# A two-layer graph kernel: adjacency and code transposes moved from TensorE to DMA, and idle ticks behind the last gather

## The chip, the core and the metric

The kernel runs on one core of a Trainium2 chip. The metric is device time in microseconds (us), the median of several executions. One execution was also profiled; lines in the fences marked `profile` come from it. The engines are TensorE (PE; its weight loads are PEld), VectorE (DVE), ScalarE (ACT), GpSimd (POOL) and SyncE (SP), which here only issues DMAs.

## What is computed

There are 16 samples of 1024 nodes with 128 features, and a symmetric 0/1 adjacency matrix for each sample. Layer 0 is masked attention, layer 1 a three-stage GraphSAGE on a thinned ("dilated") adjacency:

```python
h = relu(layernorm(x))
q, k, v = (relu(h @ W.T + b) for W, b in ...)
logits = (q @ k.T) * adj - NEG * (1 - adj)
x = x + relu((softmax(logits) @ v) @ Wo.T + bo)

h = relu(layernorm(x))
adj_d = dilate(adj, nodemask)      # row by row: rows with over 10 neighbours lose most of them
for k in (1, 2, 3):                # deg: row sums of adj_d
    h = bn(relu(l2norm((adj_d @ h / deg) @ Wr[k] + h @ Wx[k] + b[k]))); hs.append(h)
x = x + concat(hs) @ Wl + bl
```

`dilate` is sequential: a row's removals also zero the columns. The kernel doesn't run it row by row. It bounds which nodes can keep neighbours, gathers the few rows of those nodes, and solves for them. At the end it tests its own assumptions (a 0/1 matrix, symmetric, a full diagonal, few enough such nodes); if one fails, a general program computes everything. The inputs here take the fast way.

## The kernel before

**Stages.** `fast` first runs attention, one *step* for each sample (16 steps, about 21 to 777 us), then finishes the last values (to about 788 us), then layer 1's first stage (to about 930 us) and its second and third. The dilation is woven into attention.

**Order of work.** The order on each engine is written by hand, in *ticks*. A step has 48 ticks (`TICKS`). `step(i)` issues one scores matmul pair every third tick (`scores`, L697: a 128×512 f32 block of logits) and in between quarters of the values matmuls of the half sample before (`values`, L713). `pace()` counts the ticks; at each it first runs what `clock.later` put off, then advances the generators in `agenda`, each with its list of ticks from `plan`. So the lists `AT_...` (L736 to L748) say when each piece of other work is emitted. Engines run what they are given in this order, and wait on semaphores for data and for free buffers; nothing is timed at run time. The SP queue too is in order.

**Loads.** `Dilation.load(b)` (L158 to L178) loads one 128×1024 f32 block row of the adjacency into `st` by SP's queue (L166, three buffers, `ST`), and ScalarE turns it into 0/1 bf16 in `ab` with row sums (L167), then counts the zeros in a second pass (L177; VectorE, L174, for the first two samples). A sample's eight block rows are loaded one step ahead, a piece every third tick (`AT_LOAD`: the block rows at ticks 1, 7, 13, 19, 25, 31, 37, 43). A load waits only for the pass that frees its `st` buffer.

**The mirror test.** `mirrors(b)` tests that `ab` is symmetric. For block row k, `mirror` (L180) transposes the blocks (j, k), j ≤ k, on TensorE into a PSUM bank (L186, 1 to 8 blocks of 128×128 bf16), and one tick later VectorE compares the bank with block row k, blocks 0 to k (L192); `odd` receives the count of differences. Ticks: `AT_MIRRORS`, one list for even and one for odd steps; the first entry is `count_loops`.

**The gather.** For every sample, `gather` (L284 to L328) has 13 pieces: four of one-hot comparisons (L291), a small matmul for row numbers (L296), the indirect DMA of 128 adjacency rows by POOL (L301), a suffix sum by VectorE (L305, `left`), the codes (L308, fp16 128×1024), eight TensorE transposes of the codes into PSUM (L312), two ScalarE evictions into `turned` (L316), a matmul of `turned` with the one-hot matrix (L320, `pq`), and three small operations on `pq`. Ticks: `AT_GATHER`, planned in odd steps for two samples. The first of the pair transposes at tick 11 of the following even step (59 − 48), the second at tick 41 of it (89 − 48).

**Beside these**, in each step: `project` of the next sample (transposes L598, Q, K and V by L676 with evictions L677 or L599 by ScalarE from a single `pm` bank), `bound` (L221), `store` of x2 rows by POOL's indirect DMAs (L540), and from step 5 on `solve`. The x tile of sample i + 2 is loaded at the head of a step (L651) into one of five buffers, and waits for an earlier sample's stored rows.

**The end.** Two pieces of the last gather, that of sample 15, run within the ticks after attention; its other pieces and the last `solve` run as `last_of_dilation` (L899) beside layer 1's first stage: `beside1` (L1054) advances it evenly over `TICKS1` = 120 ticks, 8 for each sample. `PIECES1` (L1051) is the number of pieces to spread. In that stage SP loads the x2 tiles (L840).

Of the kernel before, what the change touches and what calls it, by code (L numbers as in the profile page):

```python
# [8 lines left out]
BF = mybir.dt.bfloat16  # L9
H16 = mybir.dt.float16  # L10
I32 = mybir.dt.int32
AF = mybir.ActivationFunctionType
# [26 lines left out]
GROUP = 4  # L39
AB = 2  # L40
ST = 3
ONE_K = 2.0 ** 40
ZERO_K = 2.0 ** 126
ROUND = 2.0 ** 23
# [36 lines left out]
class Dilation:  # L81
# [7 lines left out]
    def __init__(self, tc, adj, accT, ones, jp, identf, pool, psum, rows, rows_psum, clock):  # L89

        self.nc, self.adj = tc.nc, adj
        nc = self.nc
        self.accT, self.ones = accT, ones
        self.pick = {}
        self.pool, self.psum, self.rows, self.rows_psum, self.put_off = pool, psum, rows, rows_psum, clock.later
        own = self.pool

        def const(name, shape, dtype=F32):
            return own.tile(shape, dtype, name=name, bufs=1)

        self.identf = identf
        self.identb, self.identh = (const(f"d_id{i}", [P, P], t) for i, t in enumerate((BF, H16)))
        for t in (self.identb, self.identh):
            nc.vector.tensor_scalar(t, jp, 0.0, None, op0=OP.is_equal)
        self.up = const("d_up", [P, P], BF)
        nc.vector.tensor_scalar(self.up, jp, 0.0, None, op0=OP.is_gt)
        self.after = const("d_after", [P, P], BF)
        nc.vector.tensor_scalar(self.after, jp, 0.0, None, op0=OP.is_lt)
        nc.vector.scalar_tensor_tensor(self.after, self.identb, BIG, self.after, op0=OP.mult, op1=OP.add)
        self.onesb = const("d_ones", [P, P], BF)  # L110
        nc.vector.memset(self.onesb, 1.0)
        self.onesf = const("d_onesf", [P, P])
        nc.vector.memset(self.onesf, 1.0)
        self.half = const("d_half", [P, 1], BF)
        nc.vector.memset(self.half, 0.5)
        self.one_k = const("d_one_k", [P, 1])
        nc.vector.memset(self.one_k, -ONE_K)
        ii = const("d_ii", [P, S], I32)
        nc.gpsimd.iota(ii, pattern=[[1, S]], base=1, channel_multiplier=0)
        self.iota = const("d_iota", [P, S], H16)  # L120
        nc.vector.tensor_copy(self.iota, ii)
        mi = const("d_mi", [P, NB], I32)
        nc.gpsimd.iota(mi, pattern=[[P, NB]], base=0, channel_multiplier=1)
        self.node = const("d_node", [P, NB])
        nc.vector.tensor_copy(self.node, mi)
        self.node32 = mi
        self.node16 = const("d_node16", [P, NB], H16)
        nc.vector.tensor_copy(self.node16, mi)
        self.first = [const(f"d_first{i}", [P, NB, 2], BF) for i in range(2)]
        self.away = [const(f"d_away{i}", [P, 2, NB, 3], BF) for i in range(2)]  # L130
        self.limits = [const(f"d_limits{i}", [P, NB, 2]) for i in range(2)]
        self.neghalf = const("d_neghalf", [P, 1], BF)
        nc.vector.memset(self.neghalf, -0.5)
        for t in self.away + self.first:
            nc.vector.memset(t, 1.0)

        self.deg = const("d_deg", [P, B, NB])
        self.zeros = const("d_zeros", [P, B, NB])
        self.odd = const("d_odd", [P, B, NB])
        self.loops = const("d_loops", [P, B])  # L140
        self.sizes = const("d_sizes", [P, B, 2])
        self.used = const("d_used", [P, B])
        self.code = const("d_code", [P, B, S], H16)
        self.own = const("d_own", [P, B, P], BF)
        self.dcode = const("d_dcode", [P, B])
        self.moved = const("d_moved", [P, B])
        self.kept_deg = const("d_kdeg", [P, B])
        self.slot = const("slot", [P, B, NB], I32)
        self.A = {}
        self.tail = False  # L150

    def bank(self, shape, dtype, own=False):
# [5 lines left out]
    def load(self, b):  # L158
# [5 lines left out]
        for k in range(NB):  # L164
# [12 lines left out]
                nc.scalar.activation(junk, st, AF.Exp, scale=-ZERO_K, accum_out=zeros)  # L177
            yield  # L178

    def mirror(self, b, k):  # L180

        nc = self.nc
        ab, diag = self.A[b]
        pt = self.bank([P, NB, P], BF)
        for j in range(k + 1):
            nc.tensor.transpose(pt[:, j, :], ab[:, j, k * P:(k + 1) * P], self.identb)  # L186
        n = (k + 1) * P // 2

        def compare():

            junk = self.rows.tile([P, NB, P], BF, name="junkv", bufs=1)
            nc.vector.scalar_tensor_tensor(junk.rearrange("p a b -> p (a b)")[:, :n],  # L192
                                           pt.rearrange("p a b -> p (a b)").bitcast(I32)[:, :n], 1.0,
                                           ab[:, k, :].bitcast(I32)[:, :n], op0=OP.mult, op1=OP.not_equal,
                                           accum_out=self.odd[:, b, k:k + 1])

        self.put_off(1, compare)

    def prepare(self, b):

# [83 lines left out]
    def gather(self, b):  # L284


        nc = self.nc
        used = self.used[:, b:b + 1]
        onehot = self.pool.tile([P, NB, S], H16, name="onehot", bufs=1)
        for k in range(NB):  # L290
            nc.vector.tensor_scalar(onehot[:, k, :], self.iota, self.pick[b - b % 2][:, b % 2, k:k + 1], None, op0=OP.is_equal)  # L291
            if k % 2:
                yield
        pi = self.bank([P, 1], F32)
        for k in range(NB):
            nc.tensor.matmul(pi, onehot[:, k, :P], self.node16[:, k:k + 1], start=(k == 0), stop=(k == NB - 1))  # L296
        yield
        row = self.pool.tile([P, 1], I32, name="row")
        nc.vector.tensor_scalar(row, pi, float(b * N), None, op0=OP.add)
        rows = self.pool.tile([P, N], F32, name="rows", bufs=1)  # L300
        nc.gpsimd.indirect_dma_start(out=rows, out_offset=None, in_=self.adj.rearrange("b n m -> (b n) m"),  # L301
                                     in_offset=bass.IndirectOffsetOnAxis(ap=row[:, 0:1], axis=0))
        yield
        left = self.pool.tile([P, N], H16, name="left", bufs=1)
        nc.vector.tensor_tensor_scan(left[:, ::-1], rows[:, ::-1], rows[:, ::-1], 0.0, op0=OP.add, op1=OP.bypass)  # L305
        yield
        codes = self.pool.tile([P, N], H16, name="codes", bufs=1)
        nc.vector.scalar_tensor_tensor(codes, rows, 1023.0, left, op0=OP.mult, op1=OP.add)  # L308
        yield
        pt = self.bank([P, NB, P], H16)  # L310
        for k in range(NB):
            nc.tensor.transpose(pt[:, k, :], codes[:, k * P:(k + 1) * P], self.identh)  # L312
        yield
        turned = self.pool.tile([P, NB, P], H16, name="turned", bufs=1)
        for h in range(2):
            nc.scalar.activation(turned[:, 4 * h:4 * h + 4, :], pt[:, 4 * h:4 * h + 4, :], AF.Copy)  # L316
            yield
        pq = self.bank([P, S], F32)
        for k in range(NB):
            nc.tensor.matmul(pq, turned[:, k, :], onehot[:, k, :], start=(k == 0), stop=(k == NB - 1))  # L320
        yield
        dg = self.pool.tile([P, P], BF, name="dg")
        nc.vector.scalar_tensor_tensor(dg, pq[:, :P], used, self.identf, op0=OP.mult, op1=OP.mult,
                                       accum_out=self.dcode[:, b:b + 1])
        nc.vector.tensor_scalar(self.own[:, b, :], dg, 512.0, None, op0=OP.is_gt)
        nc.vector.scalar_tensor_tensor(self.code[:, b, :P], pq[:, :P], used, self.up, op0=OP.mult, op1=OP.mult)
        nc.scalar.activation(self.code[:, b, P:], pq[:, P:], AF.Copy, scale=used)
        yield  # L328
# [184 lines left out]
def fast(ctx: ExitStack, tc: tile.TileContext, a, out, vp):  # L513
# [127 lines left out]
    with ExitStack() as s1:  # L641
# [110 lines left out]
        def plan(gen, start, ticks):  # L752
            agenda.append((gen, [start + t for t in ticks]))

        def solve_pieces(b0, b1):
            return 9 * ITER + 3 + 13 * (b1 - b0)

        def plan_step(i):
# [6 lines left out]
            else:  # L765
                late = lambda ticks: ticks
            plan(dil.bound(i), start, late(AT_BOUND[odd]))
            plan(dil.mirrors(i), start, late(AT_MIRRORS[odd]))
            if i + 1 < B:
                plan(project(i + 1), start, late(AT_PROJECT[odd]))  # L770
                plan(load_adj(i + 1), start, late(AT_LOAD))
# [120 lines left out]
                    H[b] = enter(b)  # L892
                _advance(H[b][1])
        clock.flush()
        assert all(gen is gathering[B - 1] for gen, ticks in agenda if ticks)
        dil.tail = True
    load_x2(2)

    def last_of_dilation():  # L899

        yield from gathering[B - 1]
        yield from dil.solve(LAST, B)

    def last_stores():
# [139 lines left out]
    with tc.tile_pool(name="ps1", bufs=2, space=PSUM, reuse_waits="tile") as ps:  # L1044
# [3 lines left out]
        checks = dil.verdict(a["nodemask"], vp, recips)  # L1048
        _advance(checks)

        tick, TICKS1, PIECES1 = 0, 8 * (B - 1), 13 + solve_pieces(LAST, B)  # L1051
        entering = iter(())

        def beside1():  # L1054
# [776 lines left out]
```

## Time and profile before

| | us |
|---|---|
| median of 3 runs | 1245.71 |
| lowest and highest | 1243.62 and 1247.72 |
| the profiled execution | 1249.27 |
| its span, first to last instruction | 1247.5 |
| TensorE busy in the span | 1101.4 (88%) |
| VectorE, ScalarE, POOL busy | 881.2, 727.6, 576.8 |
| transposes of adjacency blocks (L186), 576 of them | each 0.22 from start to end |
| transposes of codes (L312), 128 of them | each 0.22 to 0.31 |

How to read it: a line of the profile names engine, source line, operation, the tile written `<-` the tiles read, shapes and a count. In a timeline the first two numbers are start and duration, and `[x <-E]` says that the engine had been idle for x us until E. Consecutive matmuls overlap, so the spacing of their starts, not their durations, tells what they cost. Busy time is an average over stages with different limits; what a change in one stage is worth is read from that stage.

### The profile page before, as it was taken

The numbers are of one execution on the slowest core, as the hardware profiler recorded it, in microseconds if no ns is written. First come the engines' busy times: TensorE is split into PE (matmuls) and PEld (weight loads), VectorE is DVE, ScalarE is ACT, GpSimd is POOL, SyncE is SP. The second block draws the span as 40 slices with busy tenths as digits, with TensorE's granted clock in tenths as the row PEclk, the third lists the DMA queues.
The fourth block names the chain that finished last, engine by engine and source line by source line (L and its number), as shares of the span: only waits on it lengthen the run. The fifth ranks groups of instructions, "written<-read, shape, count | busy, mean of one in ns | idle before, by whom it ended". The sixth has DMA issues, their size and how long they took to land. (4 is left out here: it accounts for less than half of the span.)

```text
span 1247.5 us, 22348 instructions
## 1 busy us (share of the span) xinstructions
PE 1101.4 (88%) x7775; PEld 824.0 (66%) x7775; DVE 881.2 (71%) x2630; ACT 727.6 (58%) x1570; POOL 576.8 (46%) x1082
## 2 busy tenths in 40 slices
PE   4899899899899899899899798498769969999895
PEld 2567677566576676676566566477647858888673
DVE  5767568588788578678778778489866875666542
ACT  5578678677677777677677642266534542333221
POOL 0330752662652752752743605778300004777686
PEclk9899999999999999999999999699879989999797
DMA  6544334334334244244234301414000013778554
GB/s 201 154 132 136 97 128 151 124 116 131 111 114 150 86 140 149 86 137 151 85 122 135 112 25 55 120 47 111 1 1 1 1 35 99 232 218 239 164 180 124
DMA packets 118147, 143.45 MB, mean 115 GB/s; under 512 B 9212, under 2 KB 94088, under 8 KB 118024
## 3 DMA queue, kind: packets, MB, share of 16 engines
q1 hardware_dynamic: 106120, 110.78, 29.7%
q0 software_dynamic: 11904, 31.15, 7.7%
q8 instruction: 63, 1.03, 0.3%
q14 instruction: 60, 0.49, 0.1%
HBM read 113.39 MB, written 28.51 MB: 114 GB/s over the span
## 5 line engine op out<-in xcount | busy, mean ns | idle before, releaser
L713 PEld LDWEIGHTS po<-vw,e 128*128 128x128 f32 x2048 | 273.2, 194 | 65.8 <-issue 65.3
L713 PE MATMUL po<-vw,e 128*128 128x129 f32 x2048 | 307.0, 284 | 0.0
L697 PE MATMUL ps<-qT,kT 128*128 128x512 f32 x512 | 271.8, 614 | 0.8 <-ACT e L699 0.8
L700 DVE TENSOR_TENSOR e<-e,ab 128x512 f32<-128x512 f32 x256 | 177.3, 694 | 112.5 <-ACT e L699 110.8
L699 ACT ACTIVATE e<-ps 128x512 f32<-128x512 f32 x256 | 153.1, 598 | 106.0 <-PE ps L697 83.3
L540 POOL DMA_INDIRECT x_d<-xt,slot x128 | 144.2, 1127 | 38.8 <-issue 35.1
L167 ACT ACTIVATE ab<-st,d_one_k 128x1024 bf16<-128x1024 f32 x128 | 146.9, 1148 | 0.3 <-DMA st<-in_adj_dram 0.3
L576 POOL TENSOR_SCALAR ln_t<-ln_st 128x8 f32<-128x8 f32 x31 | 8.1, 260 | 289.7 <-DVE ln_st L569 231.8
L177 ACT ACTIVATE junk<-st 128x1024 bf16<-128x1024 f32 x112 | 118.3, 1056 | 0.0
L540 POOL DMA_INDIRECT y_d<-y,nodes x88 | 86.4, 982 | 29.0 <-issue 28.5
L722 ACT ACTIVATE o<-po,recips 128x128 f32<-128x128 f32 x128 | 46.8, 368 | 74.7 <-DVE recips L720 74.6
L697 PEld LDWEIGHTS ps<-qT,kT 128*128 128x128 f32 x512 | 78.6, 193 | 7.6 <-issue 3.1
L954 ACT ACTIVATE sq<-po 128x512 f32<-128x512 f32 x80 | 47.7, 596 | 57.5 <-PE po L945 51.9
L1000 ACT ACTIVATE r<-pt 128x512 f32<-128x512 f32 x74 | 44.4, 601 | 58.3 <-PE pt L988 58.3
L588 POOL TENSOR_SCALAR hn<-xt,ln 128x128 f32<-128x128 f32 x120 | 76.4, 649 | 1.6
L957 DVE TENSOR_REDUCE nrm<-sq 128x4 f32<-128x512 f32 x80 | 54.1, 676 | 31.4 <-ACT sq L954 27.8
L944 PE MATMUL po<-ws,r 128*128 128x128 f32 x512 | 75.4, 292 | 0.0
L305 DVE TENSOR_TENSOR_SCAN left<-rows 128x1024 f16<-128x1024 f32 x16 | 38.1, 2384 | 51.4 <-DMA rows<-in_adj_dram,row 51.4
L944 PEld LDWEIGHTS po<-ws,r 128*128 128x128 f32 x512 | 64.8, 198 | 12.8 <-issue 11.2
L1130 POOL COPY mark<-y 128x1 f32<-128x1 f32 x30 | 5.8, 193 | 145.8 <-DVE y L1005 143.0
L997 DVE BATCH_NORM_STATS2 stats<-r 128x6 f32<-128x512 f32 x74 | 50.9, 688 | 29.6 <-ACT r L1000 29.2
L588 POOL TENSOR_SCALAR hn<-xt 128x128 f32<-128x128 f32 x112 | 56.3, 514 | 27.0 <-PE pt L598 26.2
(300 smaller groups left out, 2435.2 us busy)
## 6 DMA issues: line engine op xcount, KB each, us to landing
st<-in_adj_dram SPq DMA_DIRECT2D x128, 512.0 KB
r<-y_d SPq DMA_DIRECT2D x22, 512.0 KB
xt<-x_d SPq DMA_DIRECT2D x16, 524.0 KB
xt<-in_x_dram SPq DMA_DIRECT2D x16, 512.0 KB
x<-x_d SPq DMA_DIRECT2D x16, 512.0 KB
out_dram<-r SPq DMA_DIRECT2D x11, 512.0 KB
x_d<-xt,slot POOLq DMA_INDIRECT x128
y_d<-y,nodes POOLq DMA_INDIRECT x88
```

Of the source, the lines that this page charges most:

```text
L167: nc.scalar.activation(ab[:, k, :], st, AF.Exp, bias=self.one_k, scale=ONE_K, accum_out=self.deg[:, b, k:k + 1])
L177: nc.scalar.activation(junk, st, AF.Exp, scale=-ZERO_K, accum_out=zeros)
L540: d = nc.gpsimd.indirect_dma_start(out=dst, out_offset=bass.IndirectOffsetOnAxis(ap=slots, axis=0), in_=src, in_offset=None)
L588: engine.tensor_scalar(hn[:, k, :], xt[:, k, :D], minus[:, k // 2, k % 2, None], rstd[:, k // 2, k % 2, None], op0=OP.add, op1=OP.mult)
L697: nc.tensor.matmul(p, K[b][:, k * P:(k + 1) * P], Q[b][:, c], start=True, stop=True)
L699: later(1, lambda: nc.scalar.activation(e, p, AF.Exp))
L700: later(2, lambda: nc.vector.tensor_mul(e, e, AB_[b][:, k, c]))
L713: nc.tensor.matmul(po[:, q % 2, :], E[k][:, i * P:(i + 1) * P], V[b][:, k, :], start=(k == 0), stop=(k == NB - 1))
L944: nc.tensor.matmul(po[:, i, :], hT[:, c:c + P], wxk, start=(i == 3), stop=False)
L954: later(1, lambda: nc.scalar.activation(sq, halves[g], AF.Square))
L957: nc.vector.tensor_reduce(n[:, 0, 4 * g:4 * g + 4], sq, axis=AX.X, op=OP.add)
L997: nc.vector.bn_stats(stats[:, 2 * b + g, :], d)
```

## The change

The transposes leave TensorE for DMA transposes that SP issues.

- `turn_rows`, a new generator, issues one DMA transpose for each block row k. It reads blocks (k, 0..k) of `ab` and writes their transposes into a `mirrored` tile, of which there are three (`MIRRORS`). It runs at the ticks of `AT_MIRRORS` less six. `mirror` then only compares, one tick later than its old entry: blocks 0..k of `mirrored` with blocks (0..k, k) of `ab`, from SBUF.
- In `gather`, one DMA transpose of `codes` into `turned` stands for the eight TensorE transposes and the two evictions. The number of pieces stays 13.
- For the last gather, `GATHER_IDLE` puts 6, 5 and 3 idle ticks (pieces that do nothing) behind the pieces numbered 5 (row numbers and indirect DMA), 7 (codes) and 8 (transpose), counted from 0. `gather_left` holds how many of its pieces are left after attention, and `PIECES1` counts these, the idle ones and those of `solve`.
- The fp16 identity matrix goes.

In the order that the changed program is built in, SP's queue holds in an odd step (b: block rows in the transpose; ticks in brackets) `st`[1], 1b[7], `st`[7], 2b[10], 3b[13], `st`[13], 4b[16], 5b[19], `st`[19], 6b[23], `st`[25], 7b[27], `st`[31], 8b[35], `st`[37], `st`[43], and in an even step `st`[1], `st`[7], codes[11], `st`[13], 1b[14], 2b[17], `st`[19], 3b[23], `st`[25], 4b[27], 5b[29], `st`[31], 6b[33], 7b[36], `st`[37], 8b[38], codes[41], `st`[43]. A transpose into `mirrored` waits for the compare three before it. VectorE's operations keep their order.

```diff
+MIRRORS = 3
...
+    def turn_rows(self, b):
+
+        nc = self.nc
+        ab = self.A[b][0]
+        for k in range(NB):
+            pt = self.rows.tile([P, NB, P], BF, name="mirrored", bufs=MIRRORS)
+            nc.sync.dma_start(pt[:, :k + 1, :], ab[:, k, :(k + 1) * P], transpose=True)
+            self.mirrored.append(pt)
+            yield
+
     def mirror(self, b, k):
 
-        nc = self.nc
-        ab, diag = self.A[b]
-        pt = self.bank([P, NB, P], BF)
-        for j in range(k + 1):
-            nc.tensor.transpose(pt[:, j, :], ab[:, j, k * P:(k + 1) * P], self.identb)
-        n = (k + 1) * P // 2
-
-        def compare():
-
-            junk = self.rows.tile([P, NB, P], BF, name="junkv", bufs=1)
-            nc.vector.scalar_tensor_tensor(junk.rearrange("p a b -> p (a b)")[:, :n],
-                                           pt.rearrange("p a b -> p (a b)").bitcast(I32)[:, :n], 1.0,
-                                           ab[:, k, :].bitcast(I32)[:, :n], op0=OP.mult, op1=OP.not_equal,
-                                           accum_out=self.odd[:, b, k:k + 1])
-
-        self.put_off(1, compare)
+        pt = self.mirrored.pop(0)
+        junk = self.rows.tile([P, NB, P], BF, name="junkv", bufs=1)
+        self.nc.vector.scalar_tensor_tensor(junk[:, :k + 1, :].bitcast(I32), pt[:, :k + 1, :].bitcast(I32), 1.0,
+                                            self.A[b][0][:, :k + 1, k * P:(k + 1) * P].bitcast(I32), op0=OP.mult,
+                                            op1=OP.not_equal, accum_out=self.odd[:, b, k:k + 1])
...
-        pt = self.bank([P, NB, P], H16)
-        for k in range(NB):
-            nc.tensor.transpose(pt[:, k, :], codes[:, k * P:(k + 1) * P], self.identh)
-        yield
         turned = self.pool.tile([P, NB, P], H16, name="turned", bufs=1)
-        for h in range(2):
-            nc.scalar.activation(turned[:, 4 * h:4 * h + 4, :], pt[:, 4 * h:4 * h + 4, :], AF.Copy)
-            yield
+        nc.sync.dma_start(turned, codes, transpose=True)
+        yield
+        yield
+        yield
...
-            plan(dil.mirrors(i), start, late(AT_MIRRORS[odd]))
+            plan(dil.turn_rows(i), start, late([t - 6 for t in AT_MIRRORS[odd][1:]]))
+            plan(dil.mirrors(i), start, late([t + (j > 0) for j, t in enumerate(AT_MIRRORS[odd])]))
...
-        assert all(gen is gathering[B - 1] for gen, ticks in agenda if ticks)
+        (gather_left,) = (len(ticks) for gen, ticks in agenda if ticks)
...
+    GATHER_IDLE = {5: 6, 7: 5, 8: 3}
+
     def last_of_dilation():
 
-        yield from gathering[B - 1]
+        for part in range(13 - gather_left, 13):
+            next(gathering[B - 1])
+            for _ in range(1 + GATHER_IDLE.get(part, 0)):
+                yield
         yield from dil.solve(LAST, B)
...
-        tick, TICKS1, PIECES1 = 0, 8 * (B - 1), 13 + solve_pieces(LAST, B)
+        tick, TICKS1, PIECES1 = 0, 8 * (B - 1), gather_left + sum(GATHER_IDLE.values()) + solve_pieces(LAST, B)
```

More of the change, by code (lines that the diff above doesn't have):

```diff
@@ L101, in __init__ @@
         self.identf = identf
-        self.identb, self.identh = (const(f"d_id{i}", [P, P], t) for i, t in enumerate((BF, H16)))
-        for t in (self.identb, self.identh):
-            nc.vector.tensor_scalar(t, jp, 0.0, None, op0=OP.is_equal)
+        self.identb = const("d_id", [P, P], BF)
+        nc.vector.tensor_scalar(self.identb, jp, 0.0, None, op0=OP.is_equal)
         self.up = const("d_up", [P, P], BF)
@@ L149, in __init__ @@
         self.A = {}
+        self.mirrored = []
         self.tail = False
@@ L309, in gather @@
         yield
-        pt = self.bank([P, NB, P], H16)
-        for k in range(NB):
-            nc.tensor.transpose(pt[:, k, :], codes[:, k * P:(k + 1) * P], self.identh)
+        turned = self.pool.tile([P, NB, P], H16, name="turned", bufs=1)
+        nc.sync.dma_start(turned, codes, transpose=True)
         yield
-        turned = self.pool.tile([P, NB, P], H16, name="turned", bufs=1)
-        for h in range(2):
-            nc.scalar.activation(turned[:, 4 * h:4 * h + 4, :], pt[:, 4 * h:4 * h + 4, :], AF.Copy)
-            yield
+        yield
+        yield
         pq = self.bank([P, S], F32)
```

## The prediction

> **What bounds the kernel now.** I read the page first: engine totals, then the slices. TensorE is the busiest engine, and in the attention stage (about 21 to 780 us) its slices are at eight or nine tenths.
>
> ```profile
> PE 1101.4 (88%) x7775; PEld 824.0 (66%) x7775; DVE 881.2 (71%) x2630; ACT 727.6 (58%) x1570; POOL 576.8 (46%) x1082
> ```
>
> Next, busy time by windows, one for each sample step, cut where a step's first scores matmul (L697) starts. An even step (sample 8, here) comes before an odd one (sample 9). Columns: stretch, length, then each engine's busy time.
>
> ```profile
> 392.90:439.50 46.60, 41.82 (x292) 29.02 (x291) 30.75 (x86) 33.63 (x66) 22.45 (x45) 1.00 0.39 118
> 439.50:484.20 44.70, 44.32 (x330) 31.79 (x329) 35.41 (x130) 36.01 (x69) 24.04 (x45) 1.00 0.42 138
> ```
>
> The odd step leaves TensorE 0.4 us idle: TensorE bounds it. The even step leaves 4.8 us idle: something else ends last there. The wait view of that window, TensorE only (total, times, longest), names its largest stall:
>
> ```profile
> PE pm L676 <- ACT qT L677: 2.0, 1, 2.0
> ```
>
> The timeline shows where it comes from. VectorE sits idle 6.2 us for the gathered rows, then scans them, then does the fourth mirror compare:
>
> ```profile
> 424.35 2.29 DVE L305 TENSOR_TENSOR_SCAN left<-rows 128x1024 f16<-128x1024 f32 x1 [6.23 <-DMA rows<-in_adj_dram,row]
> ...
> 427.15 0.41 DVE L192 SCALAR_TENSOR_TENSOR junkv<-pd,ab 128x256 bf16<-128x256 int32 x1
> ```
>
> ScalarE waits behind that, then evaluates an adjacency block row (L167) ahead of the qT eviction:
>
> ```profile
> 427.69 0.37 ACT L722 ACTIVATE o<-po,recips 128x128 f32<-128x128 f32 x1 [4.02 <-DVE recips L720]
> ...
> 428.69 1.16 ACT L167 ACTIVATE ab<-st,d_one_k 128x1024 bf16<-128x1024 f32 x1
> ...
> 429.82 0.70 ACT L677 ACTIVATE qT<-pm,c_L_gnn_bq 128x512 f32<-128x512 f32 x1
> ```
>
> TensorE's K projection waits for that eviction; from there to the next step's first scores TensorE has no gap, and the transposes are part of that stretch:
>
> ```profile
> 430.57 1.13 PE L676 MATMUL pm<-hT,w_L_gnn_Wk 128*128 128x512 f32 x2 [1.95 <-ACT qT L677]
> ...
> 431.98 0.61 PE L312 MATMUL pd<-d_id,codes 128*128 128x128 f16 x8
> ...
> 435.54 0.61 PE L186 MATMUL pd<-d_id,ab 128*128 128x128 bf16 x8
> ...
> 439.52 1.02 PE L697 MATMUL ps<-qT,kT 128*128 128x512 f32 x2
> ```
>
> [...] eight take 0.61 us with the 0.22 us of the last one, so (0.61 − 0.22)/7 = 56 ns apart; I use 57. No DMA transpose is in this trace. [...] SyncE waits up to 18.8 us at the x load (L651), and the next adjacency loads (L166) leave only once it has gone:
>
> ```profile
> 435.74 0.38 SPq L651 DMA_DIRECT2D xt<-in_x_dram  x1
> 436.21 4.81 SPq L166 DMA_DIRECT2D st<-in_adj_dram  x3
> ```
>
> [...]
>
> **The change, part by part.**
>
> *Removed from TensorE:* 36 block transposes for each sample, 36 × 57 ns = 2.05 us, and 8 for the codes, 0.46 us; 16 samples, 40 us in all. Also the wait for codes (L312), 11.5 us over eight places in attention. ScalarE loses two 0.6 us evictions for each sample. VectorE's compare keeps its shape (0.21 to 0.69 us) and its order; costed at nothing, since only its source moves from PSUM to SBUF.
>
> *Added to SyncE:* nine transposes for each sample[...]; the order is what matters. Three `mirrored` buffers mean that transpose k waits for compare k−3, and the adjacency loads emitted after it wait behind it. Now those loads run far ahead: SyncE's timeline has the three for ticks 31, 37 and 43 leaving between 407.4 and 416.1.
>
> A load's own time: the one issued at 445.51 has gone by 448.6, 3.1 us later (windows of 1 us; the second but last column is the DMA share):
>
> ```profile
> 447.50:448.50 1.00, 1.00 (x10) 0.95 (x9) 0.92 (x3) 0.76 (x2) 0.81 (x3) 1.00 0.87 352
> 448.50:449.50 1.00, 1.00 (x14) 0.48 (x13) 0.53 (x2) 0.19 (x1) 0.70 (x4) 1.00 0.03 12
> ```
>
> *Even step.* The build order puts the load for tick 37 behind the transpose of block row 6, which waits for compare 3. That compare ends at 427.56. [...] ScalarE wants it at 428.69, so L167 is 3.9 us late, with it the qT eviction and TensorE's K projection. After 430.57 TensorE has 15 mirror blocks and the codes less to do, 0.86 + 0.46 = 1.3 us. Net +2.6 us. What TensorE saves ahead of the stall (21 blocks, the codes at tick 11, the wait for them) buys nothing: the stall ends by the gather, which POOL issues behind its own normalization. Seven even steps (2 to 14): +18.2 us.
>
> *Odd step.* The load for tick 19 stands behind the transpose of block row 4, which waits for compare 1:
>
> ```profile
> 455.14 0.28 DVE L192 SCALAR_TENSOR_TENSOR junkv<-pd,ab 128x128 bf16<-128x128 int32 x1
> ...
> 456.73 1.14 ACT L167 ACTIVATE ab<-st,d_one_k 128x1024 bf16<-128x1024 f32 x1
> ...
> 459.15 0.60 ACT L599 ACTIVATE hT<-pm 128x512 f32<-128x512 f32 x1 [0.34 <-PE pm L598]
> ...
> 461.18 1.10 PE L676 MATMUL pm<-hT,w_L_gnn_Wq 128*128 128x512 f32 x2
> ```
>
> [...] 3.3 us after 456.73. Then L167 with its accumulator read (1.35), one exponential (0.6) and the hT eviction (0.6): TensorE's Q projection at 462.55 in place of 461.18, +1.4; the 26 blocks after it save 1.5. Net −0.1; seven such steps −0.7. Step 15 loads nothing and keeps its full 2.05. Step 0 and step 1: nothing counted.
>
> *The idle ticks.* Now TensorE stands 12.1 us in layer 1 for codes that hang on the last gather:
>
> ```profile
> 797.07 1.07 POOL L301 DMA_INDIRECT rows<-in_adj_dram,row  x1 [0.16 <-issue]
> ...
> 802.21 3.81 DVE L305 TENSOR_TENSOR_SCAN left<-rows 128x1024 f16<-128x1024 f32 x1 [8.75 <-DMA rows<-in_adj_dram,row]
> ...
> 807.40 1.03 PE L312 MATMUL pb<-d_id,codes 128*128 128x128 f16 x8 [12.12 <-DVE codes L308]
> ```
>
> The gather lands at 802.2 still, and the scan then holds VectorE to 806, with sample 0's scaling behind it. So the turn of sample 0 (tick 13) can't come before about 807.5; before, TensorE was at tick 7 then. Six ticks of about 1.1 us (142 us over 128 ticks): −6.5 us. The same pieces in fewer ticks give about 0.5 us back: −6. The turned codes queue ahead of only later x2 loads: nothing.
>
> *Sum:* 18.2 − 0.7 − 2.05 − 6 = +9.4 us. The profiled execution took 1249.27 us (span 1247.5, 1.8 around it), so 1258.7 for such a one; it lies 3.6 above the median 1245.71. On the median: **1255 us**.
>
> **Bounds of the unknown price.** Low: a transpose holds SyncE like a plain load, 0.33 us. Even 427.56 + 0.33 + 3.1 − 428.69 − 1.3 = +1.0, odd −1.3: 7 × (1.0 − 1.3) − 2.05 − 6 = −10, so 1236. High: [...] Even +4.1, and the load for tick 43 behind two 8-block transposes adds about 0.9; odd +0.9: 7 × 5.9 − 8 = +33, so 1279. A gain below nothing for SyncE is excluded: it only gets work.
>
> **Rivals.** (a) [...] the high bound, 1279. [...] Against: the x load's 1,024 short rows cost SyncE only 0.38 us against 0.33 for the 128 of an adjacency load. (b) *SyncE is hardly held:* the low bound, **faster, 1236**. One mechanism: SyncE's time in the transposes ahead of the loads for ticks 19 and 37. Even is c + 0.7 and odd 0.76c − 1.6 for a 7-block time c; with the other −8, the sign turns at c = 1.2 us. (c) *The loads aren't late:* compares come early enough, or the ScalarE delay is swallowed, since it idles about 9 of 45 us a step. Then odd steps give 8 × 2.05, even ones 7 × 1.3, layer 1 gives 6: −31.5, so 1214. Against: the Q and K projections wait for ScalarE one for one. (d) *Nothing moves,* if gains and stalls cancel: the stretch between (b) and my forecast.
>
> **How the numbers follow.** Forecast 0.38 (own range 1248 to 1266), (a) 0.14, (b) 0.28, (c) 0.20; (d) lies inside the first and third. A difference under 0.3% (3.7 us) is about what a measurement of this kernel can't tell from none. Slower: (a) and most of the forecast, 0.50; same 0.10; faster 0.40. Range 1218 to 1282: it leaves out the lower half of (c) and the end of (a).
>
> **What would show it.** In the changed profile: SyncE's wait view with the transposes waiting for the compares and adjacency loads late behind them; L167's successor idle for its own load, about 4 us in even and 3 us in odd steps; SyncE's duration of one transpose (1.5 to 2 us as forecast); even steps about 49 us, odd about 44.6; the 12.1 us wait in layer 1 gone. ScalarE without waits for its loads and odd steps near 42.5 us would prove me wrong.

## The result and the profile after

The changed kernel takes **1289.7 us**, median of four runs (1287.95 to 1290.92), against 1244.7 before; the ratio is 1.0354, 95% interval 1.0335 to 1.0372. I had forecast 1255, with a range up to 1282: the side was right, the size was not. Forecast +9.4 us, measured +45 on the medians and +38.7 on the two profiled spans (1247.5 to 1286.2).

The engine totals of the changed kernel come first. TensorE did lose its work, 27.7 us of busy time, and its share of the span fell from 88% to 83%: the time is not in what it does but in what it waits for.

```profile
PE 1073.7 (83%) x7071; PEld 792.6 (62%) x7071; DVE 877.3 (68%) x2629; ACT 710.0 (55%) x1538; POOL 576.4 (45%) x1082
```

Busy time by windows for the whole attention stage (first scores of step 0 to first scores of step 15). The kernel before:

```profile
21.40:729.60 708.20, 656.18 (x4590) 457.77 (x4590) 523.09 (x1731) 519.97 (x1000) 325.55 (x630) 0.98 0.40 124
```

and the changed kernel, with samples 8 (even) and 9 (odd) below it; columns as in the prediction (the seventh number after the length is the granted TensorE clock):

```profile
21.30:782.60 761.30, 639.25 (x3937) 435.51 (x3937) 521.33 (x1731) 504.42 (x972) 326.50 (x630) 0.93 0.54 144
...
422.10:474.80 52.70, 40.95 (x241) 27.55 (x240) 30.84 (x86) 32.06 (x63) 23.81 (x45) 0.90 0.62 157
474.80:519.80 45.00, 42.13 (x294) 29.51 (x293) 34.79 (x130) 35.42 (x69) 24.31 (x45) 1.00 0.49 140
```

Attention is 53.1 us longer, and TensorE's idle time in it grew by 70 us, from 52 to 122. Two numbers are to be seen here: the even step went from 46.6 to 52.7 us, and the clock from 0.98 to 0.93, which the forecast had no term for.

SyncE's waits, even step 8 of the changed kernel (total, times, longest). Its transposes wait for the codes and for compares:

```profile
SPq L311 <- DVE codes L308: 13.5, 1, 13.5
SPq L187 <- DVE junkv L195: 11.3, 2, 9.6
```

Compare 3 (four blocks; 0.42 us with its source in SBUF, 0.41 before with it in PSUM) ends at 456.69 on VectorE's timeline:

```profile
456.27 0.42 DVE L195 SCALAR_TENSOR_TENSOR junkv<-mirrored,ab 128x256 int32<-128x256 int32 x1
```

SyncE's timeline in that step, where `x2` merges two transposes with the wait between them. The second of the two at 446.33 waits for that compare, and the load for tick 37 leaves behind it, at 458.04:

```profile
444.22 0.53 SPq L167 DMA_DIRECT2D st<-in_adj_dram  x1
446.33 11.62 SPq L187 DMA_TRANSPOSE mirrored<-ab  x2
458.04 0.53 SPq L167 DMA_DIRECT2D st<-in_adj_dram  x1
458.67 1.23 SPq L187 DMA_TRANSPOSE mirrored<-ab  x1
```

ScalarE's timeline in the same stretch: it stands 4.49 us for that load and evicts qT only then (forecast 3.9):

```profile
457.57 0.37 ACT L719 ACTIVATE o<-po,recips 128x128 f32<-128x128 f32 x1
462.43 1.15 ACT L168 ACTIVATE ab<-st,d_one_k 128x1024 bf16<-128x1024 f32 x1 [4.49 <-DMA st<-in_adj_dram]
463.48 0.19 ACT L168 ACTIVATION_READ_ACCUMULATOR ab<-st,d_one_k 128x1 f32 x1
463.58 0.67 ACT L674 ACTIVATE qT<-pm,c_L_gnn_bq 128x512 f32<-128x512 f32 x1
```

TensorE's timeline: idle 8.15 us where it was 1.95, and then two K projection matmuls take 2.07 us where the same two took 1.13 before; later, at 473.46, they are back at about 1.0:

```profile
464.30 2.07 PE L673 MATMUL pm<-hT,w_L_gnn_Wk 128*128 128x512 f32 x2 [8.15 <-ACT qT L674]
...
467.02 1.91 PE L694 MATMUL ps<-qT,kT 128*128 128x512 f32 x2
...
473.46 1.02 PE L673 MATMUL pm<-hT,w_L_gnn_Wv 128*128 128x512 f32 x2
```

The windows of this stretch name the reason. The clock falls to half at about 460, four us into the idle time, and comes back at 470.4, six us after work began again:

```profile
457.00:459.00 2.00, 0.00 (x0) 0.00 (x0) 1.52 (x4) 0.94 (x3) 1.70 (x2) 1.00 0.66 143
...
460.00:462.00 2.00, 0.00 (x0) 0.00 (x0) 0.00 (x0) 0.00 (x0) 1.39 (x3) 0.53 0.98 275
...
466.00:468.00 2.00, 2.00 (x7) 1.32 (x6) 0.00 (x0) 0.69 (x1) 0.00 (x0) 0.50 0.35 91
...
471.00:473.00 2.00, 2.00 (x14) 1.35 (x14) 0.60 (x3) 1.28 (x2) 0.00 (x0) 1.00 0.99 272
```

When the clock falls can be read from the traces. In that of the kernel before and in that of the changed one, all changes of the clock lie on a grid of 3.41 us, and the half-speed stretches in the changed kernel's attention last 3.4 us (ten of them), 6.8 (seven) or 10.2 (two): one, two or three windows of that grid. The stall of 1.95 us in step 8 of the kernel before left the clock at 1.00.

A window need not be empty for it. I counted the windows of the grid in the sixteen steps of both kernels, from the clock records and TensorE's instructions (shares are rough, as the ends of matmuls are modelled). Of those at full clock in which TensorE was busy for under 40%, all 23 were followed by one at half clock; between 40% and 70% it was 3 of 36, above that none of 360. From half clock none of the 10 windows busy under 80% led back to full clock, and all 26 busy 90% or more did. So 60% of a window, about 2.0 us of idle time, was enough where it fell into one window, and a stall of over 4.1 us must leave one window that idle wherever it falls (an estimate from these counts).

In odd step 7 another chain carries the late load. These are lines of four engines' timelines, SyncE, ScalarE, VectorE and TensorE:

```profile
384.72 4.36 SPq L187 DMA_TRANSPOSE mirrored<-ab  x2
389.18 0.53 SPq L167 DMA_DIRECT2D st<-in_adj_dram  x1
```

```profile
393.14 1.15 ACT L168 ACTIVATE ab<-st,d_one_k 128x1024 bf16<-128x1024 f32 x1 [5.25 <-DMA st<-in_adj_dram]
```

```profile
394.90 0.69 DVE L697 TENSOR_TENSOR e<-e,ab 128x512 f32<-128x512 f32 x1 [5.88 <-ACT e L696]
...
396.42 0.15 DVE L236 TENSOR_TENSOR d_away<-pd,d_limits 128x2 bf16<-128x2 f32 x1
```

```profile
396.63 0.16 PE L233 MATMUL pd<-d_away,ab 128*128 128x2 bf16 x1 [4.92 <-DVE d_away L236]
...
396.68 2.06 PE L673 MATMUL pm<-hT,w_L_gnn_Wq 128*128 128x512 f32 x2
```

ScalarE late means the exponential late, so VectorE's multiplication, and behind it in VectorE's order the small `d_away` on which `bound`'s matmuls (L233) stand, ahead of the Q projection that I had watched.

### The profile page after: what moved, and what is told of

The parts are those of the page before. It is cut to its first block, busy times and chain, and to the rows that moved or that the text cites. A ratio compares the mean times of both kernels' runs of the same rounds, so it can differ in the third digit from the quotient of the medians.

```text
span 1286.2 us, 21170 instructions
## 1 busy us (share of the span) xinstructions
PE 1073.7 (83%) x7071; PEld 792.6 (62%) x7071; DVE 877.3 (68%) x2629; ACT 710.0 (55%) x1538; POOL 576.4 (45%) x1082
## 4 chain that ended last, share of the span: by engine, by line
PE 46%; DVE 23%; DMA 11%; POOL 8%; ACT 7%; issue 4%; SPq 1%; POOLq 0%; DVEq 0%; ACTq 0%
PE po L710 8%; PE ps L694 8%; DMA st<-in_adj_dram 7%; PE po L948 6%; PE pm L673 5%; DVE e L697 4%; DMA rows<-in_adj_dram,row 3%; PE pt L992 3%; PE ph L1159 2%; ACT ab L168 2%; PE ph L1160 2%; POOL hn L585 2%; DVE left L305 2%; PE pm L681 2%; DVE m L359 2%
## 5 line engine op out<-in xcount | busy, mean ns | idle before, releaser
L710 PEld LDWEIGHTS po<-vw,e 128*128 128x128 f32 x2048 | 280.6, 200 | 82.5 <-issue 79.1
L694 PE MATMUL ps<-qT,kT 128*128 128x512 f32 x512 | 275.8, 623 | 0.8 <-ACT e L696 0.8
L537 POOL DMA_INDIRECT x_d<-xt,slot x128 | 147.0, 1148 | 48.5 <-issue 45.9
L719 ACT ACTIVATE o<-po,recips 128x128 f32<-128x128 f32 x128 | 46.9, 369 | 78.5 <-DVE recips L717 78.5
L694 PEld LDWEIGHTS ps<-qT,kT 128*128 128x128 f32 x512 | 81.8, 200 | 6.6 <-ACT e L696 2.8
L673 PE MATMUL pm<-hT,w_L_gnn_Wk 128*128 128x512 f32 x60 | 39.4, 744 | 49.1 <-ACT qT L674 49.1
L233 PE MATMUL pd<-d_away,ab 128*128 128x2 bf16 x448 | 31.1, 165 | 46.4 <-DVE d_away L236 45.8
```

The lines of the kernel that those rows point to most:

```text
L537: d = nc.gpsimd.indirect_dma_start(out=dst, out_offset=bass.IndirectOffsetOnAxis(ap=slots, axis=0), in_=src, in_offset=None)
L673: nc.tensor.matmul(pp, w, hT[:, 512 * g:512 * g + 512], start=True, stop=True)
L694: nc.tensor.matmul(p, K[b][:, k * P:(k + 1) * P], Q[b][:, c], start=True, stop=True)
L710: nc.tensor.matmul(po[:, q % 2, :], E[k][:, i * P:(i + 1) * P], V[b][:, k, :], start=(k == 0), stop=(k == NB - 1))
```

## The experiments

The runs are spread over four chips, each of which ran the kernel before too: 1 to 4 on chip A, 5 to 7 and the first of 8 on chip B, 9 to 12 on chip C, 13 to 15 and the second of 8 on chip D. The kernel before takes 1287 us on A and on B and 1247 us on C and on D, near the 1245 of the result, so ratios are compared, and step lengths only within a chip or between chips with like times. "Last exponential" is the start of attention's last ScalarE exponential, counted from the span's start.

**1. Loads two ahead.** The order of SyncE's queue is changed, and nothing else (`AHEAD` is 2):

```diff
-            st = self.rows.tile([P, N], F32, name="st", bufs=ST)
-            nc.sync.dma_start(st, self.adj[b, k * P:(k + 1) * P, :])
+            while self.issued <= min(b * NB + k + AHEAD, B * NB - 1):
+                n = self.issued
+                self.st.append(self.rows.tile([P, N], F32, name="st", bufs=ST))
+                nc.sync.dma_start(self.st[-1], self.adj[n // NB, n % NB * P:(n % NB + 1) * P, :])
+                self.issued += 1
+            st = self.st.pop(0)
```

> Theory (order in SyncE's queue): in the changed kernel the adjacency loads stand behind transposes that wait for compares and for the codes; ScalarE gets its block rows late (82 us of waits), TensorE stalls for up to 8 us at a time and its granted clock then falls to 0.5. Here each load is issued two block rows ahead, so ahead of those transposes. If that is the cause, ScalarE's waits for st fall from 82 to under 10 us, the half-clock stretches in attention from 51 us of lost clock to near the 12 of before, and the time is 1215 to 1225 us. Rival (traffic): the 104,000 small packets slow the loads themselves, whatever the order; then loads still land late and the time stays at 1270 or more.

Measured 0.9738 (0.9690 to 0.9786) of the kernel before. The changed kernel itself, on chip B (run 5), has 1.0349: the same transposes, the same bytes, in another order, are 6% faster. ScalarE's waits for `st` are gone from its list. The clock recovers only in part, not to near the 12 us that I expected: summed over the attention, time × (1 − granted clock) is 32 us here, 61 in the changed kernel on chip B and 17 with the idle ticks alone there (51 in the changed kernel and 12 in the kernel before where both were first profiled).

**2. A buffer for each transpose.**

```diff
-            pt = self.rows.tile([P, NB, P], BF, name="mirrored", bufs=MIRRORS)
-            nc.sync.dma_start(pt[:, :k + 1, :], ab[:, k, :(k + 1) * P], transpose=True)
+            pt = self.rows.tile([P, k + 1, P], BF, name=f"mirrored{k}", bufs=1)
+            nc.sync.dma_start(pt, ab[:, k, :(k + 1) * P], transpose=True)
```

> Each of the eight transposes of a sample has a buffer of its own, so none waits for a compare; the wait of the codes' transpose ahead of loads stays. Theory (order in the queue): the odd steps and the long stalls ahead of the K projection go, the loads behind the codes stay late in even steps: 1225 to 1245 us. Rival (traffic): 1280 or more, as the transposes move the same bytes.

Measured 0.9786 (0.9736 to 0.9837), better than expected. Taking away the waits for compares is nearly as good as moving the loads, though the codes' transpose still stands ahead of loads (ScalarE waits 29.9 us for them, 14 times).

**3. Both edits.**

> Loads two ahead and a buffer for each transpose. Theory (order): no more than the loads ahead give alone, since those already stand ahead of every wait: 1212 to 1222 us, within 4 us of that kernel. Rival (traffic): 1270 or more. Rival (late compares, VectorE held by waits for transposes): clearly faster than loads ahead alone.

Measured 0.9752 (0.9701 to 0.9802), the same as the first. Compares that wait for transposes are not a further cost that these runs can show; in run 1 VectorE waits for transposes 2.7 us in all.

**4. Transposes that nobody reads.** The kernel before with the idle ticks, plus `turn_rows` as in the changed kernel, its output unused.

> The kernel before with the idle ticks, its TensorE transposes kept, and the 128 DMA transposes of block rows issued where the changed kernel issues them into three buffers that nobody reads: SyncE's hold and the traffic alone, without a wait for compares or codes. Theory (order): little price, the idle ticks give some 13: 1230 to 1242 us. Rival (traffic or SyncE's time): the attention loses most of its 53 us here too, 1265 or more.

Measured 0.9945 (0.9922 to 0.9968). The idle ticks alone have 0.9933 on chip B, and the last exponential starts at 789.5 us here and at 789.7 there. So 128 transposes in SyncE's queue, with 78,000 added small packets and a DMA share of 0.56 against 0.38, cost the attention nothing that shows between these two chips when none of them waits for a compare (the two intervals leave room for some 5 us). Traffic as the cause of the loss is out. SyncE's own time per transpose in this kernel, from the list of that tile's instructions (ns, least, median and largest):

```profile
L187 SPq DMA_TRANSPOSE mirrored<-ab x128: 1119/1220/2822, 34.1 to 751.4; - x128
```

**5. The changed kernel again.**

> The changed kernel itself once more, on the chip of the next three, so that the parts are set against it and the kernel before on one chip. Both theories: 1.035 times the kernel before.

Measured 1.0349 (1.0282 to 1.0415), where the result has 1.0354.

**6 and 7. One part at a time**, each with the idle ticks: only `gather`'s edit (codes), or only `turn_rows` and `mirror` (block rows).

> Only the codes are turned by DMA (with the idle ticks); the adjacency blocks stay on TensorE. Theory (order in SyncE's queue): one transpose for each sample, that in even steps stands ahead of the loads for ticks 13 to 25 and waits up to 14 us for the codes; the idle ticks give 13, TensorE's wait for codes goes, but even steps lose some 2 us each: 0.990 to 1.000 times before (1233 to 1245 us where before takes 1245). Rival (traffic): with an eighth of the transposes gone only few packets remain (one instruction in nine), so about 0.985.

> Only the adjacency blocks are turned by DMA (with the idle ticks); the codes stay on TensorE. Theory (order): the waits for compares ahead of loads remain, so most of the attention's loss of 53 us does, some 40, less 13 from the idle ticks: 1.015 to 1.030 times before. Rival (the codes' wait is the main block): 1.005 or less.

Measured 0.9956 (0.9937 to 0.9974) for the codes and 1.0406 (1.0332 to 1.0480) for the block rows. The first is as expected and level with the idle ticks alone, so it gains nothing of its own. The second is worse than I expected and no better than the whole change: SyncE's long wait for the codes, which I had come to suspect from the trace as a main block, is not one. The loss comes with the block rows.

**8. Idle ticks alone**, run on chips B and D.

> The kernel before with the idle ticks alone, all transposes on TensorE. The idle ticks empty TensorE's wait of 12 us for the last codes and the half clock behind it: 0.988 to 0.991 times before (1230 to 1234 us), and nothing changes in the attention. Rival (the 14 us saved behind the attention come from the turned codes, not from the ticks): within 3 us of before.

> The idle ticks alone once more, on the chip of these four. The forecast's account (six ticks saved): 0.995 times before. With the half clock that TensorE has during and behind the wait of 12 us in the kernel before (6.8 us lost there): 0.989 to 0.992.

Measured 0.9933 (0.9911 to 0.9955) and 0.9952 (0.9937 to 0.9968), that is −6.0 us of 1246.65 on chip D, the forecast's −6, and −8.6 of 1287.3 on chip B: less than the larger values that I expected after the result. The wait for the last codes shrinks but stays, in the list of TensorE's waits on chip D:

```profile
PE pb L312 <- DVE codes L308: 5.4, 1, 5.4
```

**9. No block rows turned.** The compare reads the block column in both places.

```diff
-            nc.sync.dma_start(pt[:, :k + 1, :], ab[:, k, :(k + 1) * P], transpose=True)
-            self.mirrored.append(pt)
+            self.mirrored.append(ab[:, :, k * P:(k + 1) * P])
```

> The changed kernel without the 128 transposes of block rows: each compare reads the block column itself in both places (so the test of symmetry is left out); codes by DMA, idle ticks as in the changed kernel. It is what taking the transposes off TensorE could give at best. Theory (order in SyncE's queue): the kernel with the loads two ahead (0.974 times before) has nearly all of it: 0.965 to 0.978. Rival (traffic or the compares from SBUF cost as well): 0.955 or less.

Measured 0.9847 (0.9819 to 0.9875), slower than expected, and slower than the next kernel, which does turn them. It was no ceiling: loads behind the codes' transpose were left as they were, and ScalarE still waits 31 us for them. Run 14, the same with its loads ahead, has 0.9798 on chip D, so standing behind the codes costs some 6 us (an estimate across two chips with like times).

**10. Loads two ahead, codes on TensorE.**

> The loads two ahead, block rows turned by DMA, but the codes on TensorE. Theory (order): the loads stand ahead of all waits here too, TensorE has 8 blocks more for each sample and waits for codes: 0.976 to 0.984 times before, slightly behind the 0.974 of the loads ahead with both moved. Rival (the codes' wait in SyncE's queue still costs): 0.970 or less.

Measured 0.9799 (0.9763 to 0.9834), as expected. The codes' transposes and their evictions are back on TensorE and ScalarE here, so the gain beyond that of the idle ticks comes with the block rows.

**11 and 12. A stall made by hand** in the kernel before, in even steps only, by n extra ScalarE passes ahead of the qT eviction (n is 2, then 6):

```diff
+        def hold(i):
+            for _ in range(n):
+                nc.scalar.activation(dil.rows.tile([P, N], BF, name="junk", bufs=1), dil.A[i][0][:, 0, :], AF.Copy)
+            yield
...
+            if i and not odd:
+                plan(hold(i), start, [36])
```

> The kernel before, all transposes on TensorE, no idle ticks; in the seven even steps 2 to 14 ScalarE gets two more passes of 1.05 us ahead of the qT eviction that TensorE's K projection waits for (extra work, nothing left out). The forecast's account, one for one: TensorE's wait grows from 2.0 to 4.1 us, 7 x 2.1 = 15 us, 1.012 times before. [...]

> As the last, with six passes: TensorE's wait grows from 2.0 to 8.3 us. One for one: 7 x 6.3 = 44 us, 1.034 times before. With the half clock behind each stall (6.8 us at half speed, 3.4 lost, of which some falls into the stall itself): 55 to 70 us, 1.043 to 1.054.

Measured 1.0131 (1.0096 to 1.0167), +17 us where 15 are one for one, and 1.0437 (1.0404 to 1.0469), +54 us where 44 are. The first sum hides two effects. In steps 6 and 14 the two passes found room and delayed the K projection by under 0.2 us, so the seven steps lost 9.9 us up to it and 8.2 behind it: the stalls of 4.0 us in steps 4 and 8 already left half clock behind them, at 1.7 us each. TensorE's wait in step 8 of run 12 is that of the changed kernel, without a single DMA transpose:

```profile
PE pm L676 <- ACT qT L677: 8.3, 1, 8.3
```

and the windows of that step show the same half clock, in and behind it:

```profile
456.00:458.00 2.00, 0.00 (x0) 0.00 (x0) 0.00 (x0) 1.94 (x3) 0.00 (x0) 0.50 0.10 34
458.00:460.00 2.00, 0.00 (x0) 0.00 (x0) 0.42 (x1) 2.00 (x5) 0.00 (x0) 0.50 0.44 128
460.00:462.00 2.00, 1.76 (x2) 0.84 (x3) 1.17 (x3) 1.71 (x4) 0.00 (x0) 0.50 1.09 374
462.00:464.00 2.00, 2.00 (x14) 1.83 (x13) 0.00 (x0) 0.69 (x1) 0.00 (x0) 0.50 0.65 182
```

From the K projection to the next step's first scores, with the same work, the mean of the seven even steps is 11.0 us here against 9.2 before: **1.8 us** for each such stall beyond the stall itself. (Starts read from TensorE's timeline, steps 2 to 14.) In six of the seven steps the extra is half of the half-clock time that lies behind the projection, within 0.1 us: 3.3 us gives 1.6 in step 2, 4.95 gives 2.4 in step 4, 4.2 gives 2.0 in step 8. Step 12 has less extra because the kernel before pays there too: its stretch takes 10.7 us, with 3.4 of them at half clock, where steps 2, 4, 8 and 10 take 8.95. So the half clock, and not ScalarE's lateness, is the price.

**13 to 15. Control, ceiling, and the first once more**, on one chip: the kernel before with idle ticks and loads ahead; the changed kernel with loads ahead and no block rows turned; and with loads ahead alone.

> Control: the kernel before with the idle ticks and the loads two ahead, all transposes on TensorE. If the gain of the kernels with the loads ahead (0.974 to 0.980) comes from TensorE's relief, this one has the idle ticks' gain alone: 0.988 to 0.993 times before. Rival (the earlier loads themselves make up the gain): 0.980 or less.

> No transposes of block rows at all (each compare reads the block column itself; the test of symmetry is left out), codes by DMA, loads two ahead, idle ticks: the ceiling. Theory (order): SyncE's transposes cost nothing once the loads stand ahead of them, so it equals the kernel with the loads ahead within 0.004. Rival (DMA traffic and compares that wait for it cost several us): faster than that kernel by over 0.006.

> The changed kernel with the loads two ahead once more, on one chip with its ceiling and its control. Theory (order): 0.972 to 0.980 times before, faster than the control by 0.010 or more. Rival (the traffic): no faster than the control.

Measured 0.9968 (0.9950 to 0.9986), 0.9798 (0.9760 to 0.9836) and 0.9818 (0.9773 to 0.9863); the first and the last lie a little above the ranges that I expected. The third lies 0.002 from its ceiling, and 0.015 below the control: loads ahead alone give nothing, TensorE's relief gives 19 us once they are ahead. Windows of this kernel, attention as a whole, sample 9 and sample 8:

```profile
22.30:711.20 688.90, 623.49 (x3935) 426.24 (x3935) 521.16 (x1731) 502.65 (x969) 336.67 (x630) 0.96 0.62 159
429.90:472.90 43.00, 41.95 (x293) 29.45 (x292) 34.83 (x130) 35.34 (x68) 24.67 (x45) 1.00 0.62 161
...
383.00:429.90 46.90, 39.70 (x241) 26.85 (x240) 30.65 (x86) 31.94 (x63) 23.81 (x45) 0.96 0.64 162
```

This odd step gains 1.7 us against the kernel before. This even step gains nothing, 46.9 against 46.6, though TensorE does 2.1 us less: it is not TensorE that bounds it. Over steps 2 to 14 the means are 48.8 us for even steps, against 49.9 in the control on the same chip, and 43.2 for odd ones against 45.1.

## Why the prediction was right in its side and wrong in its size

Each step is cut in two at the forecast's own point, TensorE's first K projection behind the stall (even steps) or first Q projection (odd steps), and the two kernels are compared from the start of the step to it, and from it to the next step. In us:

| part | forecast | measured |
|---|---|---|
| steps 0 and 1 | 0 | +5.5 |
| even 2 to 14, up to the K projection | 7 × 3.9 | 7 × 4.5 |
| even, behind it | 7 × −1.3 | 7 × +0.6 |
| odd 3 to 13 (the forecast counted seven, there are six), up to the Q projection | 6 × 1.4 | 6 × 2.5 |
| odd, behind it | 6 × −1.5 | 6 × −0.5 |
| step 15, to its last exponential | −2.05 | −1.5 |
| what follows | −6 | −12.9 |

**The mechanism held.** The loads for ticks 37 and 19 stand behind transposes that wait for compares 3 and 1, and ScalarE is late by about what the sum said. Runs 1 and 2 remove the cause in two ways, and the loss goes with it both times.

**The step that failed is "After 430.57 TensorE has 15 mirror blocks and the codes less to do ... Net +2.6 us".** It took the stall one for one and the work behind it at full speed. In step 8 the idle time of 8.15 us brought the clock down to 0.50, and what followed ran at that for six us. Run 12 prices this apart, 1.8 us a stall. With that the even step's −1.3 becomes +0.5; measured +0.6. Likewise in odd steps: 3, 9 and 11, without half clock behind the Q projection, have −1.6, −1.5 and −1.5 behind it, where the forecast had −1.5; steps 5, 7 and 13, with 3.4, 5.4 and 3.4 us of it, have +0.1, +1.6 and +0.1. Together that is 7 × 1.9 + 6 × 1.0 = 19 of the 29 us that the profiled spans missed the forecast by; for the odd steps' part no run isolates it. It is read from the clock: half of those times on top of −1.5 gives +0.2, +1.2 and +0.2. The rest of the 29 is +11 up to the projections, +5.5 in steps 0 and 1, and −7 behind the attention. The trace before gave the hint: from 800 to 810, during and behind its 12 us wait in layer 1, the granted clock was 0.50, and eight code transposes took 1.03 us there where eight in attention took 0.61, both in lines that the prediction quotes; and step 12 there already took 10.7 us behind its K projection where step 8 took 8.95.

**"SyncE's duration of one transpose (1.5 to 2 us as forecast)": wrong, 1.2 whatever the number of blocks** (medians in the changed kernel run from 1.12 us for one block to 1.23 for eight), so below all of my values but the low bound. The 1.5 to 2 us, and that more blocks take longer, were the author's estimate, which no trace of before shows; the forecast's 3.9 us of lateness in even steps, its 3.3 in odd ones and its high bound rest on it. At c = 1.2 the forecast's own account says no change (rival (b)'s break-even). The errors next to it were larger and of the other sign, so that the kernel got slower as forecast was in part luck.

**"3.1 us" for a load: mis-sized.** I had read it off the DMA share. The list of DMA issues has the time to landing, where the profile has it: 3.7 us median in the kernel with idle ticks alone (chip D), and in the changed one

```profile
st<-in_adj_dram SPq DMA_DIRECT2D x128, 512.0 KB, 4.5
```

The transposes beside it account for some 0.8 of the 1.4 missing at most. With 4.5 for the load and 1.2 for the transpose, the forecast's own sums up to the projections give 4.6 in even steps (427.56 + 1.2 + 4.5 − 428.69) and 2.5 in odd ones: the measured means of 4.5 and 2.5. The forecast's path was right, its two durations were off in opposite directions. Single odd steps scatter from 1.4 to 4.4; step 7, with the chain through `d_away` that the forecast didn't have, is the 4.4.

**"Step 0 and step 1: nothing counted": wrong**, +3.8 and +1.8 by the starts of their scores. They too load behind transposes; I didn't follow their chains.

**The idle ticks: right in size on chip D.** Run 8 has −6.0 there, and −8.6 on chip B; the 12.1 us wait is not gone with them, as the forecast had it, but 5.4. The other 6 us saved behind the attention come in every kernel of chips C and D whose block rows leave TensorE (what follows the last exponential takes 463 to 466 us in these four, the two that turn no block rows among them, against 470 with idle ticks alone and 477 in the kernel before), whether or not the codes move. They don't come on chips A and B: 484 to 487 us in four such kernels with 484 for the idle ticks alone, and 480 in the changed kernel itself. In run 10, TensorE's wait for the last codes is down to 1.7 us. Why the gather is earlier against TensorE there I didn't trace.

**Rival (c), 1214 us, "the loads aren't late", is what the change gives when its loads are put ahead**: 0.974 to 0.982 of 1245.7 is 1213 to 1223. That its total fits is in part luck: against the control the even steps give 1.1 us and the odd ones 1.9, where it had 1.3 and 2.05, and what follows the attention gives 13.5 us against the kernel before, where it had 6. Its odd steps near 42.5 us came true at 43.2. The changed kernel as given is the worse of two orders of the same work.

## What to carry to other kernels

Before work is moved to a queue, list what stands behind it there and what it will wait for: SyncE's queue passed each wait on to what stood behind it (in step 8 a transpose's 9.6 us for a compare, to the load for tick 37), and prefetched loads lost their lead although the queue had time to spare (nine transposes of 1.2 us and eight loads of 0.52 are some 15 us of a 51 us step, an estimate from these medians). Put the loads ahead of what waits, or give what waits its own buffers; either turned +3.5% into −2%. And price a TensorE stall by more than its length: here those of 1.95 us cost themselves, those of 4.0 us 1.7 more and those of 8.3 us 1.6 to 2.4 more, half of the half-clock time behind them. So look at the clock column beside and behind each long wait.

## What was not expected of the hardware

- A DMA transpose from SBUF to SBUF held SyncE for 1.2 us whether it had one block of 128×128 bf16 or eight (medians 1.12 and 1.23 in the changed kernel), against 0.33 us for a plain load of 512 KB in the kernel before (0.52 in the changed one). It landed after 2.9 us (median) in the changed kernel and 3.5 in the one with loads ahead.
- Such transposes moved in small packets: 104,000 packets under 512 bytes in the changed kernel against 9,000 before; the DMA share of attention rose from 0.40 to 0.54, and in run 4, where it is 0.56, no cost showed.
- Chips differ by 3% for the kernel before, 1247 us on two and 1287 on two others. In the kernel with idle ticks alone, the odd steps 3 to 13 take 43.6 to 46.3 us on chip D and 45.4 to 50.6 on chip B, the even ones no more on B than on D in the mean; I found no cause in the traces.
- TensorE's clock fell to half not only after idle windows: in attention, being busy for under 40% of one 3.41 us window was enough, 23 times of 23 in the kernel before and the changed one.
